# Decoder layer: feed-forward integers transposed by DMA, cross scores on four row tiles

## The chip, the cores and the metric

The kernel runs on one core of a Trainium2 chip. The metric is the device time of one execution in microseconds; the time before is the median of three runs. The core's engines are named as in the profile: PE (TensorE; PEld is its weight load), DVE (VectorE), ACT (ScalarE), POOL (GpSimd) and SP (SyncE, which issues most DMAs). PSUM is the memory PE writes to; it is used here as eight banks of 128 partitions by 512 floats.

## What is computed

One decoder layer for 32 sequences of 256 tokens and 256 features, in float32, with the norm after each residual sum:

```python
x = layernorm(x + self_attention(x))        # 16 heads of 64, 4 key/value heads, rotary, ALiBi, no mask
x = layernorm(x + cross_attention(x, ctx))  # 16 heads of 16, windows of 64 tokens, cell mask
x = layernorm(x + feed_forward(x))          # 256 -> 1024 -> 256, quantised
```

In cross attention the query in window w sees keys of the windows w-1 and w that lie not after it and have the same cell number. The scores of a head contract over only 16 features. In the feed-forward both operands of each product are quantised: the activations are scaled by 127 over the row's largest absolute value and rounded to whole numbers, the weights are rounded to -1, 0 and 1. Whole numbers up to 127 are exact in bfloat16, so these three products run in bfloat16.

```python
scale = 127.0 / clip(max(abs(x), axis=-1, keepdims=True), 1e-05)
xq = clip(round(x * scale), -128.0, 127.0) / scale
gate = silu(bitlinear(x, w_gate)); up = bitlinear(x, w_up)
return bitlinear(gate * up, w_down)
```

## The kernel before

All weights, rotary tables and the ALiBi rows are loaded once and stay on the core. The work is cut by batch (sequence), and each batch into many small parts, written as Python generators (`self_inputs`, `self_output`, `cross_inputs`, `cross_output`, `feed_forward`) and unit functions (`self_scores`, `self_turn`, `self_values`, `cross_scores`, `cross_exp`, `cross_turn`, `cross_values`, `cross_back`). A loop at the end of the kernel (L891 to L945) walks over "slots": two slots are a step, a batch has eight steps (16 slots), and in each slot every running generator goes on to its next `yield`; `yield 2` means "go on two slots later". So three batches are in work at a time: while the self scores of batch b run, batch b-1 is in its cross attention and feed-forward and batch b+1 has its inputs projected.

The order on PE, DVE and ACT is exactly the order in which the loop records the instructions. The orders on POOL and on SP are set by the scheduler. Each engine works its own instructions in order; a waiting instruction holds up all behind it.

PSUM tiles come from one pool of eight banks (`bank(...)`). A new tile takes over the bank that has been free longest, so its first writer waits for the last reader of the tile before. SBUF tiles come from `work(name, shape, bufs)`; with `bufs` 1 the next writer waits for the last reader of the one buffer.

The parts that the change touches:

- `cross_scores` (L648). A unit is one half of the query tokens (`qc`, 128 rows) and one half of the features (`ch`, 8 heads of 16). The features of 8 heads lie on 128 partitions. The keys stand in `kTz`, which is block diagonal: in each group of 64 partitions (4 heads) the key of head j stands in column block j, zeros elsewhere (`XHH` is 4). One matmul of 64 rows thus gives the scores of 4 heads side by side, 4 x 128 columns, in one bank. The two groups of 64 partitions are two row tiles of the PE array. Query half 0 sees 128 keys (2 matmuls of 128 queries). Query half 1 is two windows with different keys: 4 matmuls of 64 queries, two row by two column tiles. Eight DVE reductions (L668) then add the mask and find the row maxima. There are four units per batch, one in every second step.
- `cross_inputs` (L570), whose end (L637 to L640) copies the rotated keys into `kTz` by eight small DMAs. `kTz` is zeroed once, in `prepare_buffers` (L170).
- `feed_forward` (L766). POOL scales x2 and adds a large constant, which rounds (L783); DVE subtracts it and writes bfloat16 `xib` (L785). In the next slot PE transposes it in four blocks (L790) and ACT copies the result from PSUM to `xiT` (L794); in the slot after that the gate products start (L802). ACT's tanh (L816) and DVE (L817, L823) make the gated product in `gu`. For each half of the tokens (t = 0, 1) DVE finds the row maximum (L829) and the scales, POOL rounds (L838), and one slot later DVE writes the bfloat16 numbers into the lower part of `gu` itself (L843). One slot after the second of these, PE transposes half 0 in eight blocks (L849), ACT copies it (L851), and one slot later the down product runs (L855). Half 1 follows one slot behind that. Then the residual, the statistics, the norm and the store (L859 to L864).
- On SP's queue, in this order within a batch: the two copies inside `xvaug` (L631, L632), the next `xT` (L112), a rotary exchange `other<-psin` (L313, four DMAs each), the eight `kTz` copies (L640), an exchange `other<-qb` (L555), `ck_i` (L576), the residual input `xs` (L320), more exchanges, the store (L195) and the next context `cs` (L574).
- Other names used below: `s` and `p`, self scores and their softmax (L394, L410, L420); `t` and `pT`, its transpose and ACT's copy of it (L447, L452); `o`, values; `wo`, output product, added to the residual by DVE in L505 (`row`); `R`, the broadcast reciprocals; `proj`, projections (L331); `xt`, `xpT`, `xo`, `xoT`, the same for cross attention; `zoT` and `zT` (L205, L206), the transposed input of the cross output product `xw` (L755).

Of the kernel before, what the change touches and what calls it, by code (L numbers as in the profile page):

```python
# [9 lines left out]
F32 = mybir.dt.float32  # L10
BF16 = mybir.dt.bfloat16
I32 = mybir.dt.int32
AF = mybir.ActivationFunctionType
ALU = mybir.AluOpType
AX = mybir.AxisListType

P = 128
L = 256
# [32 lines left out]
def kernel(  # L51
# [33 lines left out]
    def ctile(shape, dtype, name):  # L85
        return const.tile(shape, dtype, name=name, tag=name)
# [3 lines left out]
    def bank(name, shape=(P, 512), dtype=F32):  # L90
        return ps.tile(list(shape), dtype, tag="b", name=name)
# [67 lines left out]
        t = ctile([P, (NT + 1) * XH * XE + 32 - XE], F32, f"xvaug{i}")  # L159
        xvaug_bufs.append(t)  # L160

    kTz = ctile([P, NDC, XHH, L], F32, "kTz")

    def prepare_buffers():
        nc.gpsimd.tensor_copy(cq_sb, cq_i)
# [404 lines left out]
    def cross_inputs(b):  # L570

        s = state[b]
        cs = work("cs", [P, NT, D], 1)
        nc.sync.dma_start(cs, cx[b].rearrange("(t p) d -> p t d", p=P))  # L574
        ck_i = work("ck_i", [P, L], 1, I32)
        nc.sync.dma_start(ck_i, cell_k[b].partition_broadcast(P))  # L576
        yield 4
        mvs = [stats(cs[:, t, :], "zc") for t in range(NT)]
        rstds = [rstd_of(mv, "zc") for mv in mvs]
        yield  # L580
        zc = cs
        for t in range(NT):
            last.append(partial(scaled, zc[:, t, :], cs[:, t, :], rstds[t]))
        ck = work("ck", [P, L], 1)
        nc.gpsimd.tensor_copy(ck, ck_i)
        yield 2
        zcT = work("tr", [P, NDC, L], 3)
        for t in range(NT):
            transposed(zcT[:, :, t * P : (t + 1) * P], zc[:, t, :], "zcT")


        s["mask"] = mask = work("mask", [P, NT, P])
        for rows_, t, k0 in ((slice(0, P), 0, 0), (slice(0, 64), 1, 64), (slice(64, P), 1, 128)):
            nc.gpsimd.tensor_scalar(
                mask[rows_, t, :], ck[rows_, k0 : k0 + P], cq_sb[rows_, b, t : t + 1], BIG, ALU.is_equal, ALU.mult
            )
        nc.gpsimd.tensor_tensor(mask, mask, base_sb, ALU.add)
        yield
        s["xv"] = xvaug_bufs[b % 2]
        xvaug = s["xv"][:, 0 : (NT + 1) * XH * XE].rearrange("p (t h e) -> p t h e", h=XH, e=XE)  # L600
        pk = bank("xk")
        for ch in range(NDC):
            for dc in range(NDC):
                nc.tensor.matmul(  # L604
                    pk[:, ch * L : (ch + 1) * L],
                    xkv_w[:, dc, ch * P : (ch + 1) * P],
                    zcT[:, dc, :],
                    start=(dc == 0),
                    stop=(dc == NDC - 1),
                )  # L610
        pair = biased(pk, K_, L)
        yield
        pv = bank("xv")
        for t in range(NT):
            for dc in range(NDC):
                nc.tensor.matmul(  # L616
                    pv[:, t * D : (t + 1) * D],
                    zcT[:, dc, t * P : (t + 1) * P],
                    xkv_w[:, dc, D : 2 * D],
                    start=(dc == 0),  # L620
                    stop=(dc == NDC - 1),
                )
        for t in range(NT):
            nc.vector.tensor_tensor(
                xvaug[:, t, :, 0:XHD],
                pv[:, t * D : (t + 1) * D].rearrange("p (h e) -> p h e", e=XHD),
                xbias[V_].rearrange("p (h e) -> p h e", e=XHD),
                ALU.add,
            )

        nc.sync.dma_start(xvaug[0:64, NT, :, :], xvaug[64:P, 0, :, :])  # L631
        nc.sync.dma_start(xvaug[64:P, NT, :, :], xvaug[0:64, 1, :, :])  # L632
        yield
        kT = work("tr", [P, NDC, L], 3)
        rotated(kT, *pair, 1, 0)
        yield 3
        for half in range(2):  # L637
            for j in range(XHH):
                rows_ = slice(half * 64 + j * XHD, half * 64 + (j + 1) * XHD)
                nc.sync.dma_start(kTz[rows_, :, j, :], kT[rows_, :, :])  # L640


# [5 lines left out]
    def cross_scores(b, i):  # L648
        s = state[b]
        qc, ch = cross_units[i]  # L650
        banks = [bank("xs") for _ in range(2)]
        for q0, q1, k0, _t in spans[qc]:
            for half in range(2):
                rows_ = slice(half * 64, (half + 1) * 64)
                nc.tensor.matmul(  # L655
                    banks[half].rearrange("p (h k) -> p h k", k=P)[q0:q1],
                    s["xqT", qc][rows_, ch, q0:q1],
                    kTz[rows_, ch, :, k0 : k0 + P],
                    start=True,
                    stop=True,  # L660
                )
        s["xnm", i] = [small("xnm", 4) for half in range(2)]
        for half in range(2):
            s["xp", i, half] = p = work("xp", [P, 512])
            for j in range(XHH):
                cols = slice(j * P, (j + 1) * P)

                nc.vector.tensor_tensor_reduce(  # L668
                    p[:, cols],
                    banks[half][:, cols],  # L670
                    s["mask"][:, qc, :],
                    -1.0,
                    3.0e38,
                    ALU.add,
                    ALU.min,
                    s["xnm", i][half][:, j : j + 1],
                )
# [88 lines left out]
    def feed_forward(b):  # L766
# [16 lines left out]
            nc.gpsimd.tensor_scalar(xi[:, t, :], x2[:, t, :], up[:, t : t + 1], MAGIC, ALU.mult, ALU.add)  # L783
        yield
        nc.vector.tensor_scalar(xib, xi, MAGIC, None, ALU.subtract)  # L785
        yield
        pt = bank("xiT", (P, NDC, L), BF16)
        for dc in range(NDC):
            for t in range(NT):
                nc.tensor.transpose(  # L790
                    pt[:, dc, t * P : (t + 1) * P], xib[:, t, dc * P : (dc + 1) * P], ident_b
                )
        xiT = work("xiT", [P, NDC, L], 1, BF16)
        nc.scalar.copy(xiT, pt)  # L794
        yield

        gu = work("gu", [P, NT, INNER], 1)

        def hidden(name, t, half):
            pg = bank("ff")  # L800
            for dc in range(NDC):
                nc.tensor.matmul(  # L802
                    pg,
                    xiT[:, dc, t * P : (t + 1) * P],
                    ff_w[name][:, dc, half * 512 : (half + 1) * 512],
                    start=(dc == 0),
                    stop=(dc == NDC - 1),
                )
            return pg
# [9 lines left out]
        for t in range(NT):  # L819
# [2 lines left out]
                cols = gu[:, t, half * 512 : (half + 1) * 512]  # L822
                nc.vector.tensor_tensor(cols, cols, pg, ALU.mult)  # L823
            yield
        d_ofs, hibs = [], []
        for t in range(NT):

            m = small("ffm", 1)
            nc.vector.tensor_reduce(m, gu[:, t, :], AX.X, ALU.max, apply_absolute_value=True)  # L829
            sh = small("ffsh", 1)  # L830
            nc.vector.tensor_scalar(sh, m, u_of[:, t : t + 1], QUANT_MIN, ALU.mult, ALU.max)
            hup = small("ffhup", 1)
            nc.vector.reciprocal(hup, sh)
            nc.vector.tensor_scalar(hup, hup, u_of[:, t : t + 1], 127.0, ALU.mult, ALU.mult)
            d_of = small("ffd", 1)
            nc.vector.tensor_scalar(d_of, sh, ff_scale["down"], None, ALU.mult)
            d_ofs.append(d_of)
            nc.gpsimd.tensor_scalar(gu[:, t, :], gu[:, t, :], hup, MAGIC, ALU.mult, ALU.add)  # L838
            yield

            gh = gu[:, t, :].rearrange("p (h n) -> p h n", h=2)
            hib = gu[:, t, :].bitcast(BF16).rearrange("p (h x n) -> p h x n", h=2, x=2)[:, :, 0, :]
            nc.vector.tensor_scalar(hib, gh, MAGIC, None, ALU.subtract)  # L843
            hibs.append(hib)
        yield
        for t in range(NT):
            pt = bank("hiT", (P, NIC, P), BF16)
            for ic in range(NIC):
                nc.tensor.transpose(pt[:, ic, :], hibs[t][:, ic // 4, ic % 4 * P : (ic % 4 + 1) * P], ident_b)  # L849
            hiT = work("hiT", [P, NIC, P], 1, BF16)  # L850
            nc.scalar.copy(hiT, pt)  # L851
            yield
            py = bank("ffo")
            for ic in range(NIC):
                nc.tensor.matmul(  # L855
                    py[:, 0:D], hiT[:, ic, :], ff_w["down"][:, ic, :], start=(ic == 0), stop=(ic == NIC - 1)
                )
            y = x2[:, t, :]
            nc.vector.scalar_tensor_tensor(y, py[:, 0:D], d_ofs[t], y, ALU.mult, ALU.add)  # L859
            mv = stats(y, "y")  # L860
            rstd = rstd_of(mv, "y")
            yield
            last.append(partial(scaled, y, y, rstd))
# [171 lines left out]
```

## Time and profile before

| | |
|---|---|
| median of three runs | 2324.79 us (2323.94 to 2325.04) |
| profiled execution | 2327.47 us |
| its span, first to last instruction | 2325.7 us |
| mean granted PE clock | 0.987 |
| ACT, copies hiT (L851) and xiT (L794) | 64.7 + 18.7 us busy |
| DVE, cross reductions (L668) | 225.9 us busy |
| DMA engines, queue of SP and ACT | 18.7% of 16 engines |

The span is the time between the first and the last instruction of the profiled execution; all rows of the profile belong to that execution, and a sum over rows is set against it. "Busy" of a group is the time covered by its instructions, where those of one group may overlap. In a timeline row the first number is the start within the span, the second how long the instruction or merged group lasted; brackets give idle time of the engine just before and what ended it. Names such as 64*128 behind a PE row are the rows and columns of the array tile that is used; "x8" is a number of records.

### The profile page before, as it was taken

Reading aid. Unit: us, or ns where it says so; the run is one execution under the profiler, and the core shown is the slowest. Engines: PE = TensorE matmul, PEld = TensorE weight load, DVE = VectorE, ACT = ScalarE, POOL = GpSimd, SP = SyncE. Lnnn points to the kernel's source line nnn. Section 1 sums busy time; section 2 is a strip of 40 time slices with the busy share of each in tenths; the row PEclk is TensorE's granted clock in tenths of the full one; section 3 lists DMA queues with packets and bytes.
Section 4 is the critical chain, followed back from the end, with each engine's and each line's share of the span. In section 5 each row is a group of like instructions: output and inputs, shape, how many; then the busy total and the mean of one; then the engine's idle time right before and its main releaser. Section 6 shows DMA issues by size and latency. Waiting matters only on the chain.

```text
span 2325.7 us, 54754 instructions
## 1 busy us (share of the span) xinstructions
PE 2246.9 (97%) x17637; PEld 1689.2 (73%) x17700; DVE 1701.3 (73%) x6949; ACT 1764.8 (76%) x5057; POOL 1124.2 (48%) x1851
## 2 busy tenths in 40 slices
PE   7999999999999999999999999999999999999985
PEld 5677777777777777777777777777777777777652
DVE  3767777777777777777777777777777777777765
ACT  2677777878777878777878777878777878777873
POOL 5344545445545545545445545445545444545432
PEclk9999999999999999999999999999999999999996
DMA  6311211112211111211111211112211111211000
GB/s 211 87 51 47 58 53 49 47 45 52 59 52 49 47 45 53 57 51 49 47 47 54 56 51 49 47 46 54 56 51 50 46 48 53 55 47 44 20 22 10
DMA packets 105407, 123.05 MB, mean 53 GB/s; under 512 B 21792, under 2 KB 74912, under 8 KB 105120
## 3 DMA queue, kind: packets, MB, share of 16 engines
q1 hardware_dynamic: 103424, 115.96, 18.7%
q10 hardware_dynamic: 1696, 3.57, 0.4%
q8 instruction: 142, 2.33, 0.4%
q14 instruction: 145, 1.19, 0.2%
HBM read 39.50 MB, written 8.39 MB: 21 GB/s over the span
## 4 chain that ended last, share of the span: by engine, by line
PE 78%; DVE 10%; ACT 8%; issue 1%; POOL 1%; DMA 1%; SPq 0%; ACTq 0%; POOLq 0%; DVEq 0%
PE proj L331 12%; PE s L394 10%; PE wo L495 10%; PE t L447 8%; PE o L464 8%; PE xt L693 4%; ACT p L420 4%; PE xs L655 4%; DVE gu L817 3%; PE xw L755 3%; PE xv L616 3%; PE ffo L855 3%; DVE p L410 2%; PE R L479 2%; PE xk L604 2%; PE v L363 2%
## 5 line engine op out<-in xcount | busy, mean ns | idle before, releaser
L420 ACT ACTIVATE p<-p,nm 128x256 f32<-128x256 f32 x1024 | 508.0, 498 | 168.6 <-DVE nm L410 164.7
L410 DVE CUSTOM_DVE_ANT_0 p<-s,alibi 128x256 f32<-128x256 f32 x1024 | 372.7, 420 | 180.5 <-PE s L394 180.4
L452 ACT COPY pT<-t 128x512 f32<-128x512 f32 x512 | 275.2, 591 | 127.1 <-PE t L447 126.8
L684 ACT ACTIVATE xp<-xp,xnm 128x128 f32<-128x128 f32 x1024 | 326.1, 394 | 5.9 <-DVE xnm L668 5.9
L394 PE MATMUL s<-kT,qT 64*128 64x256 f32 x2048 | 290.8, 402 | 0.0
L447 PE MATMUL t<-ident,p 128*128 128x128 f32 x2048 | 269.0, 273 | 3.2 <-ACT p L420 3.2
L447 PEld LDWEIGHTS t<-ident,p 128*128 128x128 f32 x2048 | 237.9, 141 | 31.4 <-ACT p L420 6.6
L331 PE MATMUL proj<-xT,wq_sb 128*128 128x256 f32 x1024 | 251.8, 389 | 0.0
L464 PE MATMUL o<-pT,v 128*64 128x256 f32 x2048 | 250.0, 385 | 0.0
L495 PE MATMUL wo<-wo_sb,oT 128*128 128x256 f32 x1024 | 245.3, 382 | 0.0
L668 DVE CUSTOM_DVE_ANT_0 xp<-xs,mask 128x128 f32<-128x128 f32 x1024 | 225.9, 286 | 2.9 <-PE xs L655 2.1
L495 PEld LDWEIGHTS wo<-wo_sb,oT 128*128 128x128 f32 x1024 | 189.4, 190 | 47.4 <-issue 22.7
L355 POOL TENSOR_TENSOR qT<-qT,other 128x512 f32<-128x512 f32 x128 | 162.9, 1273 | 120.6 <-DMA other<-psin 53.3
L394 PEld LDWEIGHTS s<-kT,qT 64*128 64x128 f32 x2048 | 176.5, 186 | 54.7 <-issue 23.5
L340 DVE TENSOR_TENSOR psin<-proj,rs_sb 128x512 f32<-128x512 f32 x160 | 110.2, 689 | 141.7 <-PE proj L331 141.7
L331 PEld LDWEIGHTS proj<-xT,wq_sb 128*128 128x128 f32 x1024 | 186.4, 191 | 32.8 <-issue 6.4
L464 PEld LDWEIGHTS o<-pT,v 128*64 128x64 f32 x2048 | 135.7, 136 | 98.3 <-issue 22.9
L420 ACT ACTIVATION_READ_ACCUMULATOR p<-p,nm 128x1 f32 x1024 | 192.6, 188 | 0.0
L695 ACT COPY xpT<-xt 128x512 f32<-128x512 f32 x256 | 153.2, 598 | 6.1 <-PE xt L693 4.2
L693 PE MATMUL xt<-ident,xp 128*128 128x128 f32 x1024 | 154.2, 274 | 0.0
L655 PE MATMUL xs<-kTz,xqT 64*64 64x512 f32 (+1 forms) x768 | 136.6, 611 | 5.0 <-POOL xqT L568 5.0
L817 DVE SCALAR_TENSOR_TENSOR gu<-gu,ff 128x512 f32<-128x512 f32 x128 | 82.3, 682 | 72.8 <-ACT gu L816 72.8
(156 smaller groups left out, 4528.2 us busy)
## 6 DMA issues: line engine op xcount, KB each, us to landing
other<-psin SPq DMA_DIRECT2D x640, 64.0 KB, 2.0
xT<-in_xt_dram SPq DMA_DIRECT2D x32, 256.0 KB, 2.7
xs<-in_x_dram SPq DMA_DIRECT2D x32, 256.0 KB, 2.7
cs<-in_ctx_dram SPq DMA_DIRECT2D x32, 256.0 KB, 2.7
other<-qb SPq DMA_DIRECT2D x64, 128.0 KB, 2.0
kTz<-tr SPq DMA_DIRECT2D x256, 32.0 KB, 2.0
other<-qb SPq DMA_DIRECT2D x128, 64.0 KB, 1.9
out_dram<-x SPq DMA_DIRECT2D x32, 256.0 KB, 2.2
```

The source lines that it names most:

```text
L331: nc.tensor.matmul(pq[:, c * L : (c + 1) * L], w[:, dc, c * P : (c + 1) * P], xT[:, dc, :], start=(dc == 0), stop=(dc == NDC - 1),)
L394: nc.tensor.matmul(banks[half][:, rr * L : (rr + 1) * L], qT[rows_, rr, qc * P : (qc + 1) * P], kT[rows_, kc, :], start=(rr == 0), stop=(r ...
L410: nc.vector.tensor_tensor_reduce(p[:, cols], banks[half][:, cols], alibi[:, 2 * (4 * kc + 2 * rp + rr) + half, :], -0.125, 3.0e38, ALU.add ...
L420: nc.scalar.activation(p[:, cols], p[:, cols], AF.Exp, bias=nm[:, rr : rr + 1], scale=-1.0, accum_out=s["sums", i // 2][:, (2 * rp + rr) * ...
L447: nc.tensor.transpose(pt[:, j * P : (j + 1) * P], p[half][:, rr * L + kk * P : rr * L + (kk + 1) * P], ident,)
L452: nc.scalar.copy(pT[half], pt)
L464: nc.tensor.matmul(po[half * HD : (half + 1) * HD, rp * L : (rp + 1) * L], s["v"][:, kk, (2 * kc + half) * HD : (2 * kc + half + 1) * HD], ...
L495: nc.tensor.matmul(py[:, 0:D], s["oT", qc, kc][:, r, :], wo_sb[:, 4 * kc + r, :], start=(kc == 0 and r == 0), stop=(kc == 1 and r == 3),)
L655: nc.tensor.matmul(banks[half].rearrange("p (h k) -> p h k", k=P)[q0:q1], s["xqT", qc][rows_, ch, q0:q1], kTz[rows_, ch, :, k0 : k0 + P], ...
L668: nc.vector.tensor_tensor_reduce(p[:, cols], banks[half][:, cols], s["mask"][:, qc, :], -1.0, 3.0e38, ALU.add, ALU.min, s["xnm", i][half][ ...
L684: nc.scalar.activation(p[:, cols], p[:, cols], AF.Exp, bias=s["xnm", i][half][:, j : j + 1], scale=-1.0)
L693: nc.tensor.transpose(pt[:, j * P : (j + 1) * P], p[:, j * P : (j + 1) * P], ident)
```

## The change

Cross scores: `kTz` has two column blocks in place of four, and the partitions are taken in four groups of 32 (2 heads) in place of two of 64 (4 heads). Each unit takes four banks, of which each holds 2 x 128 columns, and the matmuls name their tile of the array. Query half 0 is now 4 matmuls, query half 1 is 8. The DVE reductions stay eight, and read another bank for each pair of heads. The number of `kTz` DMAs stays eight.

Feed-forward: the PE transposes of `xib` and of the quantised hidden values, with the ACT copies behind them, are replaced by DMA transposes issued on SP: two for `xib` (one per token half), one for each half of the hidden values. The gate products start in the same slot as before. The hidden numbers go to a tile of their own, `hib`, with one buffer; `hiT` has two buffers in place of one. The down product of half 1 comes one slot after that of half 0 (it was two slots).

```diff
-    kTz = ctile([P, NDC, XHH, L], F32, "kTz")
+    kTz = ctile([P, NDC, 2, L], F32, "kTz")
...
-        for half in range(2):
-            for j in range(XHH):
-                rows_ = slice(half * 64 + j * XHD, half * 64 + (j + 1) * XHD)
+        for r in range(4):
+            for j in range(2):
+                rows_ = slice(r * 32 + j * XHD, r * 32 + (j + 1) * XHD)
                 nc.sync.dma_start(kTz[rows_, :, j, :], kT[rows_, :, :])
...
-        banks = [bank("xs") for _ in range(2)]
+        banks = [bank("xs") for _ in range(4)]
         for q0, q1, k0, _t in spans[qc]:
-            for half in range(2):
-                rows_ = slice(half * 64, (half + 1) * 64)
+            for r in range(4):
+                rows_ = slice(r * 32, (r + 1) * 32)
                 nc.tensor.matmul(
-                    banks[half].rearrange("p (h k) -> p h k", k=P)[q0:q1],
+                    banks[r][:, 0 : 2 * P].rearrange("p (h k) -> p h k", k=P)[q0:q1],
                     s["xqT", qc][rows_, ch, q0:q1],
                     kTz[rows_, ch, :, k0 : k0 + P],
                     start=True,
                     stop=True,
+                    tile_position=(r * 32, q0),
                 )
...
-                    banks[half][:, cols],
+                    banks[2 * half + j // 2][:, j % 2 * P : (j % 2 + 1) * P],
...
         nc.vector.tensor_scalar(xib, xi, MAGIC, None, ALU.subtract)
-        yield
-        pt = bank("xiT", (P, NDC, L), BF16)
-        for dc in range(NDC):
-            for t in range(NT):
-                nc.tensor.transpose(
-                    pt[:, dc, t * P : (t + 1) * P], xib[:, t, dc * P : (dc + 1) * P], ident_b
-                )
-        xiT = work("xiT", [P, NDC, L], 1, BF16)
-        nc.scalar.copy(xiT, pt)
-        yield
+        xiT = work("xiT", [P, NT, NDC, P], 1, BF16)
+        for t in range(NT):
+            nc.sync.dma_start_transpose(xiT[:, t, :, :], xib[:, t, :])
+        yield 2
...
-            gh = gu[:, t, :].rearrange("p (h n) -> p h n", h=2)
-            hib = gu[:, t, :].bitcast(BF16).rearrange("p (h x n) -> p h x n", h=2, x=2)[:, :, 0, :]
-            nc.vector.tensor_scalar(hib, gh, MAGIC, None, ALU.subtract)
-            hibs.append(hib)
-        yield
-        for t in range(NT):
-            pt = bank("hiT", (P, NIC, P), BF16)
-            for ic in range(NIC):
-                nc.tensor.transpose(pt[:, ic, :], hibs[t][:, ic // 4, ic % 4 * P : (ic % 4 + 1) * P], ident_b)
-            hiT = work("hiT", [P, NIC, P], 1, BF16)
-            nc.scalar.copy(hiT, pt)
-            yield
+            hib = work("hib", [P, INNER], 1, BF16)
+            nc.vector.tensor_scalar(hib, gu[:, t, :], MAGIC, None, ALU.subtract)
+            hiT = work("hiT", [P, NIC, P], 2, BF16)
+            nc.sync.dma_start_transpose(hiT, hib)
+            hiTs.append(hiT)
+        yield 2
+        for t in range(NT):
             py = bank("ffo")
```

The gate, up and down products read `xiT` and `hiTs[t]` in place of the former tiles.

More of the change, by code (lines that the diff above doesn't have):

```diff
@@ L803, in hidden @@
                     pg,
-                    xiT[:, dc, t * P : (t + 1) * P],
+                    xiT[:, t, dc, :],
                     ff_w[name][:, dc, half * 512 : (half + 1) * 512],
@@ L824, in feed_forward @@
             yield
-        d_ofs, hibs = [], []
+        d_ofs, hiTs = [], []
         for t in range(NT):
@@ L855, in feed_forward @@
                 nc.tensor.matmul(
-                    py[:, 0:D], hiT[:, ic, :], ff_w["down"][:, ic, :], start=(ic == 0), stop=(ic == NIC - 1)
+                    py[:, 0:D], hiTs[t][:, ic, :], ff_w["down"][:, ic, :], start=(ic == 0), stop=(ic == NIC - 1)
                 )
```

## The prediction

> **What bounds the kernel now.** First the page: engine totals, and the chain that ended last.
>
> ```profile
> PE 2246.9 (97%) x17637; PEld 1689.2 (73%) x17700; DVE 1701.3 (73%) x6949; ACT 1764.8 (76%) x5057; POOL 1124.2 (48%) x1851
> ...
> PE 78%; DVE 10%; ACT 8%; issue 1%; POOL 1%; DMA 1%; SPq 0%; ACTq 0%; POOLq 0%; DVEq 0%
> ```
>
> PE is the bound, but its busy time overlaps itself (matmul ends are modelled), so I price PE work by the distance between starts in the timeline. The chain of waits shows the pace: the same projection at 1084.67 and 1154.33 us, so a batch takes 69.65 us, and 32 of them are nearly the whole span. Within a batch PE stops once, for 0.39 us (row xw below). PE timeline of one batch (start, duration; a float matmul shows as two records):
>
> ```profile
> 1046.50 1.13 PE L394 MATMUL s<-kT,qT 64*128 64x256 f32 x8
> 1047.56 1.09 PE L655 MATMUL xs<-kTz,xqT 64*64 64x512 f32 x8
> 1048.58 1.04 PE L802 MATMUL ff<-ff_up,xiT 128*128 128x512 bf16 x4
> ...
> 1052.67 1.13 PE L755 MATMUL xw<-xo_w,zT 128*128 128x256 f32 x4 [0.39 <-ACT zT L206]
> ...
> 1061.83 1.13 PE L394 MATMUL s<-kT,qT 64*128 64x256 f32 x8
> 1062.80 1.02 PE L655 MATMUL xs<-kTz,xqT 64*128 64x512 f32 x4
> 1063.75 1.99 PE L495 MATMUL wo<-wo_sb,oT 128*128 128x256 f32 x8
> 1065.68 0.65 PE L709 MATMUL xo<-xpT,xvaug 128*32 128x64 f32 x32
> 1066.26 0.62 PE L849 MATMUL hiT<-ident_b,gu 128*128 128x128 bf16 x8
> 1066.72 1.95 PE L331 MATMUL proj<-xT,wkv_sb 128*128 128x256 f32 x8
> ```
>
> **Transposes off PE.** A set of 8 hiT transposes takes 1066.72 − 1066.26 = 0.46 us; two sets are 0.92, and the four xiT take 1107.74 − 1107.52 = 0.22. Per batch 1.14, times 32: **36 us**. (The group rows say 41.1 + 12.8 = 54 us of busy time; that counts overlap.) ACT loses 64.7 + 18.7 = 83 us of copies; ACT is not the bound, so I count nothing for them.
>
> **Cross scores.** Today a unit costs 1063.75 − 1062.80 = 0.95 us (two row tiles; query half 0) or 1048.58 − 1047.56 = 1.02 (two by two tiles; half 1). Afterwards the zeros shrink from 3 in 4 to 1 in 2: four row tiles at once, each with 256 columns to stream instead of 512. No row has four row tiles. The nearest is xo, four column tiles: 8 matmuls of 128 columns, 1024 columns in all, from 1084.03 to 1084.60, 0.57 us. The new unit also streams 4 x 256 = 1024 columns over four tiles (half 1: 8 x 256 over eight). Bound from below: 0.43 (half the present stream of 0.86). From above: s, which has the same 8 records of 256 columns and full-width weights on two tiles, 0.97: no gain. I take 0.60, near xo, because weight loads of different row tiles overlap in this trace: the eight half-width loads of a half-1 unit cover only 13.4 us / 64 = 0.21 us.
>
> Against it stands a rule: the Trainium skill, "TensorEngine Tiling (Array Packing)", Key Properties: changing the tiling mode drains the array. The trace has a price: s takes 1062.80 − 1061.83 = 0.97 when xs follows in its own mode (64*128), and 1047.56 − 1046.50 = 1.06 when another follows; call it 0.10. Half 0 now gains such a switch, half 1 had it. By the pure stream the gain is 0.95 − 0.60 = 0.35; by rule and row together 0.25. So 64 x 0.25 + 64 x 0.42 = 16 + 27 = **43 us**.
>
> **What does not arrive.** (1) In the feed-forward step the 0.39 us wait above is for ACT's zT copy, at the end of a run in which DVE is full (gate and up products, then all reductions, 1044.57 to 1055.6). PE arriving 0.42 earlier there just waits longer: 0.42 x 32 = **13 us** lost. (2) The second ffo moves from after xs (1081.94) into the slot of the second hiT set (1076.38). In the step of 1080.01 PE then reaches xw 1.07 + 0.60 + 0.90 + 0.31 + 0.57 + 1.83 = 5.28 us after s; ACT's zT copy ends 1085.68 − 1080.01 = 5.67 after it. 0.39 x 32 = **12 us** lost.
>
> **The DMA transposes.** Four per batch, on SP's queue: two of 64 KB (xiT) and two of 256 KB (hiT). The trace has no such transfer. Ordinary ones:
>
> ```profile
> other<-psin SPq DMA_DIRECT2D x640, 64.0 KB, 2.0
> xT<-in_xt_dram SPq DMA_DIRECT2D x32, 256.0 KB, 2.7
> ```
>
> Price T of a hiT transfer: the Trainium skill, "DMA: Bandwidth & Descriptors", Anatomy of one DMA, puts some 2.0 us on any transfer, and its Latency section measured 261 GB/s for one kernel's transposes: 262144 B / 261 = 1.0, so 3.0 by the rule. By the trace: queue q1 moved 103424 packets in 18.7% of 16 x 2325.7 us, 67 ns each; rows of 128 elements are 1024 packets, 64 per DMA engine, 4.3 us, plus 2.0: 6.3. If it goes in pieces of 16 elements (the program's transpose tile is 16 rows by 128 columns), 512 pieces x 67 ns = 34 us. I take **4.5 us**, between the first two, and keep 3 and 34 as ends.
>
> Where it is hidden:
>
> ```profile
> 1061.02 0.70 DVE L843 TENSOR_SCALAR gu<-gu 128x1024 bf16<-128x1024 f32 x1 [0.58 <-POOL gu L838]
> ...
> 1066.63 0.69 DVE L843 TENSOR_SCALAR gu<-gu 128x1024 bf16<-128x1024 f32 x1
> 1067.24 0.42 DVE L505 TENSOR_TENSOR row<-wo,xs 128x256 f32<-128x256 f32 x1
> ```
>
> - xiT: xib ends at 1105.49, the gate matmuls start at 1112.80. Two 64 KB transfers, 0.6 us apart, at 2.0 to 3.5 us land by 1109.6: free.
> - hiT of token half 0: written by 1061.72, needed by ffo at 1073.56: free up to T = 11.8. Half 1: written by 1067.32, needed at 1076.4: 9 us.
> - The new tile hib has **one buffer**: DVE's second hib waits until the first transfer has read it. That wait has 1066.63 − 1061.72 = 4.9 us of cover. Behind it on DVE stand row L505, the reciprocals, psin and the next four p reductions; the first PE casualty is s at 1070.13, which needs the PSUM bank that row L505 frees (1067.66), 2.5 us later, some 1.8 in the shorter new schedule. So PE loses T − 6.7 per batch once T exceeds 6.7; nothing at 4.5.
> - SP: the hiT transfers come after ck_i (1056.30) and before xs (1067.68) and psin (1069.51), the xiT ones between xvaug (1104.63) and xT (1107.71): gaps of 5 us and 3 us. A psin transfer behind the second hiT may land 1 to 2 us late; the key sum that waits for it is used slots later, and POOL is 48% busy. Nothing.
>
> **PSUM.** A cross unit now takes four of eight banks. The reuse distance shrinks by two: xs's third and fourth bank wait for ACT's pT copies (end 1099.73 where xs starts 1100.44), xo in the feed-forward step for xs's first bank (freed about 1050.0; PE arrives about 1050.2). These fit, narrowly. Nothing in the sum; the loss is a rival.
>
> **End of the kernel.** In the last batch nothing covers: xib to gate is 1.3 us now, about 3.5 then (+2); first hib (ends 2311.24) to second ffo (2317.48) becomes wait 4.5, second hib 0.65, transfer 4.5: 2320.9 (+3.5). **+5.5 us**.
>
> **Sum.** 2325.7 − 36 − 43 + 13 + 12 + 5.5 = 2277 span. The profiled execution took 2327.5, 1.8 more than its span; the median is 2324.8, 2.7 below that execution. So 2278.7 − 2.7: **2276 us**, 2.1% faster.
>
> **Rivals.**
> - A, four tiles don't help: s-like loading (0.97 per unit) or four-bank waits of 0.3 to 0.4 us eat the 43 us. For: no row has four row tiles; bank slacks are tenths. Against: the overlapping loads, xo. Then the stall of (1) goes too: 2325 − 36 + 12 + 5 + 6 (the switches) = about **2310**.
> - B, slower: the transfer of hiT through one hib buffer. PE loses T − 6.7 per batch; the 49 us gain is 1.5 per batch, so it decides from T = 8.2. At T = 10: 3.3 x 32 = 106, less 49, plus 11 more at the end: about **2390**. For: small pieces are dear in this trace, the form is unseen. Against: the 64 KB and 256 KB rows at 2.0 and 2.7.
> - C, the ACT relief counts: copies of 1.01 us stand ahead of pT where o waits. If both losses (1) and (2) vanish: **2250**.
> - D, the change does not do what it says: the transposes do leave PE and the zeros halve, in every batch; only "no change by offset" remains, **2325**.
>
> **Chances.** Forecast (2250 to 2300) 0.48; C and beyond 0.05; A (2300 to 2320) 0.12; D 0.05; B and other slow cases 0.30, most of it within 2330 to 2375, a tail beyond for T over 9. A measurement of this kernel tells 0.2%, 4.7 us. Faster 0.65, same 0.05, slower 0.30. Leaving out 0.05 below and 0.15 above gives 2245 to 2375; the likeliest case alone is 2250 to 2300.
>
> **What would show it.** L790, L794, L849 and L851 gone; xs of either half near 0.6 us from start to start, with s at 1.06 before every one; a batch period near 68.1 us; DMA transposes landing in about 4.5 us; zT waits ahead of xw near 0.8 and 0.4. Wrong if: DVE's second hib shows an idle time "<-DMA hiT" of microseconds and PE waits for row L505 (B); xs near 0.9, or PE waiting for DVE xnm or ACT pT (A).

## The result and the profile after

The kernel after takes 2287.4 us in the median of four runs (2286.42 to 2288.16), against 2324.65 us: ratio 0.984, 95% interval 0.982 to 0.985. That is 37 us less, and 11 us more than the forecast of 2276.

First the page of the kernel after: engine totals, the queue that carries SP's and ACT's transfers (packets, MB, share of 16 engines), and the engines' shares of the chain that ended last.

```profile
PE 2186.2 (96%) x17828; PEld 1653.7 (72%) x17828; DVE 1709.6 (75%) x6949; ACT 1692.1 (74%) x4961; POOL 1117.3 (49%) x1851
...
q1 hardware_dynamic: 189440, 136.95, 24.3%
...
PE 71%; DVE 12%; ACT 11%; DMA 2%; issue 2%; POOL 1%; SPq 0%; ACTq 0%; POOLq 0%; DVEq 0%
```

PE's busy time fell by 61 us, the span only by 39 (2325.7 to 2286.3). The chain points to where the rest went: ACT's share grew from 8 to 11% although ACT has 73 us less to do. PE now waits longer for something that ACT does late. The PE timeline of the kernel after shows it (start, duration; in brackets idle time and its releaser):

```profile
1060.79 1.14 PE L394 MATMUL s<-kT,qT 64*128 64x256 f32 x8
1061.86 0.71 PE L656 MATMUL xs<-kTz,xqT 32*128 32x256 f32 x8
1062.50 1.16 PE L532 MATMUL xq<-zT,xq_w 128*128 128x128 f32 x8
1063.50 0.38 PE L205 MATMUL zoT<-ident,on 128*128 128x128 f32 x2
...
1064.38 1.99 PE L331 MATMUL proj<-xT,wq_sb 128*128 128x256 f32 x8
1066.57 1.13 PE L757 MATMUL xw<-xo_w,zT 128*128 128x256 f32 x4 [0.19 <-ACT zT L206]
1067.53 1.04 PE L447 MATMUL t<-ident,p 128*128 128x128 f32 x8
...
1096.82 0.73 PE L656 MATMUL xs<-kTz,xqT 32*64 32x256 f32 x16
1097.49 1.04 PE L798 MATMUL ff<-ff_up,xiT 128*128 128x512 bf16 x4
...
1100.15 1.04 PE L798 MATMUL ff<-ff_up,xiT 128*128 128x512 bf16 x4
1101.93 1.13 PE L757 MATMUL xw<-xo_w,zT 128*128 128x256 f32 x4 [0.74 <-ACT zT L206]
1102.89 1.04 PE L447 MATMUL t<-ident,p 128*128 128x128 f32 x8
```

Read it from start to start: these two cross units cost 0.64 and 0.67 us, s ahead of them 1.07. Both zT waits are there. The first of these two steps in the kernel before, for comparison:

```profile
1081.94 1.05 PE L855 MATMUL ffo<-ff_down,hiT 128*128 128x256 bf16 x8
1082.82 1.06 PE L532 MATMUL xq<-zT,xq_w 128*128 128x128 f32 x8
1083.72 0.38 PE L205 MATMUL zoT<-ident,on 128*128 128x128 f32 x2
...
1084.60 1.99 PE L331 MATMUL proj<-xT,wq_sb 128*128 128x256 f32 x8
1086.43 1.03 PE L755 MATMUL xw<-xo_w,zT 128*128 128x256 f32 x4
1087.30 1.04 PE L447 MATMUL t<-ident,p 128*128 128x128 f32 x8
```

A bracket understates such a stall. The proj group ahead of xw takes 2.19 us against 1.83 before, and xw then takes 0.96 against 0.87: 0.45 us for a bracket of 0.19. The 0.1 us in xw itself goes with its weights: without a stall they start to load 0.21 us ahead of its first matmul (kernel before), in the stall only 0.01 us ahead.

What ACT does ahead of zT in the feed-forward step (the wait at 1101.93) of the kernel after, four exponentials first:

```profile
1099.85 1.26 ACT L686 ACTIVATE xp<-xp,xnm 128x128 f32<-128x128 f32 x4
1101.02 0.60 ACT L550 ACTIVATE qb<-xq,xbcol 128x128 f32<-128x128 f32 x2
1101.52 0.36 ACT L206 COPY zT<-zoT 128x256 f32<-128x256 f32 x1
```

The period, the mean distance of the down products of 25 batches, is 68.23 us against 69.65: 1.42 us per batch, 45 us in 32 batches. Span less 32 periods leaves 97 us before and 103 after, so 6 us went back at the two ends. Step by step, from start to start, per batch:

| step of the forecast | forecast | after | one part alone |
|---|---|---|---|
| transposes and the moved ffo, off PE | -1.14 | -1.15 | transposes alone: -1.15 |
| four cross units | -1.54 | -1.37 | tiles alone: -1.36 |
| mode switch, s ahead of half 0 | +0.20 | +0.19 | tiles alone: +0.19 |
| zT wait, feed-forward step | +0.42 | +0.34 | tiles alone: +0.35 |
| zT wait in the step that ffo left | +0.39 | +0.45 | transposes alone: +0.23 |
| xq, now directly behind xs | 0 | +0.10 | transposes alone: +0.09 |
| sum | -1.67 | -1.44 (period: -1.42) | -0.83 and -0.82 |

The "one part alone" column is read from the two runs that follow. The last view of the kernel after is its DMA transposes of hiT (time on SP's queue in ns, who waited for them, landing):

```profile
L839 SPq DMA_TRANSPOSE hiT<-hib x64: 1232/1245/1860, 223.9 to 2275.1; - x64
...
  PE ffo L845: 16.6, 4
  DVE hib L837: 2.5, 2
...
DMA to landing us min/median/max: 3.0/3.1/4.8
```

A transfer of 256 KB lands after 3.1 us; those of xiT, 64 KB each, after 2.4. PE waited for hiT 4 times in the whole kernel, DVE twice, all near the end.

### The profile page after: what moved, and what is told of

Read it like the earlier page. It is cut to its first block, busy times and chain, and to the rows that moved or that the text cites. A ratio compares the mean times of both kernels' runs of the same rounds, so it can differ in the third digit from the quotient of the medians.

```text
span 2286.3 us, 55642 instructions
## 1 busy us (share of the span) xinstructions
PE 2186.2 (96%) x17828; PEld 1653.7 (72%) x17828; DVE 1709.6 (75%) x6949; ACT 1692.1 (74%) x4961; POOL 1117.3 (49%) x1851
## 3 DMA queue, kind: packets, MB, share of 16 engines
q1 hardware_dynamic: 189440, 136.95, 24.3%
## 4 chain that ended last, share of the span: by engine, by line
PE 71%; DVE 12%; ACT 11%; DMA 2%; issue 2%; POOL 1%; SPq 0%; ACTq 0%; POOLq 0%; DVEq 0%
PE s L394 10%; PE proj L331 10%; PE wo L495 9%; PE t L447 8%; PE o L464 8%; ACT p L420 4%; DVE p L410 4%; PE xt L695 4%; DVE gu L813 3%; PE xw L757 3%; ACT xp L686 3%; PE xv L616 3%; PE ffo L845 2%; PE R L479 2%; PE xk L604 2%; PE v L363 2%
## 5 line engine op out<-in xcount | busy, mean ns | idle before, releaser
L566 POOL TENSOR_TENSOR qb<-qb,rx_sb 128x256 f32<-128x256 f32 (+1 forms) x96 | 87.7, 913 | 128.9 <-ACT xp L686 76.6
```

## Experiments

Times are medians; the kernel before was run beside each and took 2324.5 to 2324.7 us.

### The two parts alone

`transposes_alone` is the kernel before with the diff of `feed_forward` only. The old kTz leaves no room for more tiles, so the new ones lie in dead parts of gu (for hib `hib_in_gu` below shows that this costs nothing):

```diff
+            hib = gu[:, 0, :].bitcast(BF16)[:, 0:INNER] if t else work("hib", [P, INNER], 1, BF16)
...
+            hiT = gu[:, t, :].bitcast(BF16)[:, INNER : 2 * INNER].rearrange("p (c q) -> p c q", q=P)
```

> The kernel before with the DMA transposes of the feed-forward alone; the cross scores stay on two row tiles. (For want of room the second hib and both hiT lie in parts of gu that are dead by then, so no transfer waits for a buffer.) Theory (the steps of the prediction, with stalls that exist only where both parts meet): PE loses 1.14 us of transposes per batch and waits for no new thing, because cross scores of the old length leave ACT's zT copy in time: 36 us gained, 5.5 given back at the end, 2294 us; ahead of xw a wait only in the feed-forward step, 0.4 us as before. Rival (the two parts do not act on each other; the shortfall against the forecast is transfer contention or the ends): the two parts' gains, this one and that of the tiles alone, add up to the 37 us of the whole change, so this one gains about 20 to 25: 2300 to 2305.

`tiles_alone` has the diff of `kTz`, `cross_inputs` and `cross_scores` only.

> The kernel before with the cross scores on four row tiles alone; the feed-forward transposes stay on PE. Theory: per batch 2 x 0.21 (query half 0) and 2 x 0.37 (half 1) of PE time go, 1.16 us, and 0.35 come back as a longer wait for ACT's zT copy in the feed-forward step; the other zT wait does not arise, because the second down product still stands in that step. 0.81 x 32 = 26 us gained: 2299 us. Alone and alone then add up to 56 us against 37 together. Rival (parts are independent): 37 less the gain of the transposes alone, about 13 to 17 us: 2308 to 2312. Rival A of the prediction (four tiles bring new waits for banks or weight loads): under 10 us gained, PE waiting for DVE xnm or ACT pT ahead of xs or xo.

Measured: transposes alone 2307.3 us (ratio 0.9925, interval 0.9912 to 0.9937), tiles alone 2302.0 (0.9902, 0.9887 to 0.9917). The gains, 17 and 22.5 us, add up to 40 against 37 together: by the times, to within their noise of some 5 us, the parts are independent, and my theory of 56 against 37 fell. It fell in the transposes alone, of which I had expected 30 us. Its PE timeline says why:

```profile
1070.22 1.13 PE L394 MATMUL s<-kT,qT 64*128 64x256 f32 x8
1071.19 1.02 PE L655 MATMUL xs<-kTz,xqT 64*128 64x512 f32 x4
1072.15 1.16 PE L532 MATMUL xq<-zT,xq_w 128*128 128x128 f32 x8
1073.14 0.38 PE L205 MATMUL zoT<-ident,on 128*128 128x128 f32 x2
...
1074.03 1.99 PE L331 MATMUL proj<-xT,wq_sb 128*128 128x256 f32 x8
1075.99 1.13 PE L755 MATMUL xw<-xo_w,zT 128*128 128x256 f32 x4
1076.96 1.04 PE L447 MATMUL t<-ident,p 128*128 128x128 f32 x8
```

The ffo that stood between xs and xq (0.88 us) has left. That alone brings PE to zT too early, with cross units of the old length: proj takes 1.96 us instead of 1.83, xw 0.97 instead of 0.87. And xq, now directly behind xs, takes 0.99 instead of 0.90. That is 0.32 us per batch, 10 us, and no PE row shows a bracket for it.

The part of xq is no wait for ACT. Directly behind xs it takes 0.99 to 1.00 us here, in the kernel after and in xs_three_units, and also in exp_later, where the steady batches have no zT wait left; behind ffo or ff it takes 0.89 to 0.90. Behind ffo its first weights start to load 0.11 us ahead of its first matmul (kernel before, 1082.71 and 1082.82), behind xs at the same moment (kernel after, 1062.50). This looks like the change of mode on its way back, but no run tests that by itself.

What the two parts do to each other is the rest of the zT stall, 0.45 − 0.23 = 0.22 us per batch, 7 us: visible in the rows, not in the medians. The first line also shows the mode switch by its absence: s takes 0.97 ahead of two row tiles, and 1.06 to 1.07 in the same place of the tiles alone.

### ACT's order ahead of zT

In ACT's order four exponentials of the cross scores stand ahead of qb and the zT copy that PE waits for. `exp_later` moves their one line, in the kernel after; `exp_later_before` does the same in the kernel before.

```diff
-            if part == 1 and not odd:
-                cross(cross_exp, k, 0)
...
             for r in list(running):
...
                         r[0] += wait or 1
+            if part == 1 and not odd:
+                cross(cross_exp, k, 0)
```

> The kernel after with one line moved: the four ACT exponentials of the first half of a cross unit (L686, 1.26 us) are recorded behind the generators' steps, so that ACT does qb and the zT copy ahead of them. Theory (PE stops per batch for 0.45 and 0.74 us because these exponentials stand before zT on ACT): zT is ready 1.2 us earlier, both waits go, 1.19 x 32 = 38 us: 2249 us, period 67.0, and no wait ahead of xw over 0.1 us. Rival (DVE, which is full in those stretches, sets the pace a little later): the waits reappear at xt, wo or s and half or less is won: 2268 to 2287.

> The kernel before with the same one line moved, as a control. Theory: there is one zT wait of 0.39 us per batch there, 12.5 us in all: 2312 us. So the edit is worth some 25 us more on the kernel after than on the kernel before, and this difference is what the change left lying in ACT's order. Rival (the edit is worth the same on both, the change did not add the waits): equal gains on both.

Measured: 2248.5 us (0.967, 0.9657 to 0.9683) and 2305.6 us (0.9915, 0.9901 to 0.9928). The edit is worth 39 us on the kernel after and 19 on the kernel before. Timelines of ACT and PE in the feed-forward step of exp_later, then, from its page, the engines' shares of the chain that ended last:

```profile
1084.85 0.60 ACT L550 ACTIVATE qb<-xq,xbcol 128x128 f32<-128x128 f32 x2
1085.35 0.35 ACT L206 COPY zT<-zoT 128x256 f32<-128x256 f32 x1
1085.60 1.29 ACT L686 ACTIVATE xp<-xp,xnm 128x128 f32<-128x128 f32 x4
```

```profile
1085.15 1.04 PE L798 MATMUL ff<-ff_up,xiT 128*128 128x512 bf16 x3
1086.03 1.03 PE L757 MATMUL xw<-xo_w,zT 128*128 128x256 f32 x4
1086.89 1.04 PE L447 MATMUL t<-ident,p 128*128 128x128 f32 x8
```

```profile
PE 90%; DVE 4%; ACT 2%; DMA 2%; POOL 1%; issue 1%; SPq 0%; ACTq 0%; POOLq 0%; DVEq 0%
```

zT now comes directly behind qb, and the exponentials after it. The chain is PE for 90% and ACT for 2%. Against the kernel after, the ff group ahead of xw takes 0.88 us instead of 1.77, proj 1.83 instead of 2.19, both xw 0.1 less; 0.24 comes back at one o. So the waits ahead of xw came from ACT's order. In the kernel before, where only the feed-forward step shows a bracket, removing its 0.39 saved 0.66 us per batch (ff 1.43 to 0.88, xw 0.97 to 0.86), which is why the control gained 19 us and not the expected 12.5. The one line makes the change worth 57 us instead of 37 (2305.6 to 2248.5), and exp_later beats both kernels.

`exp_later_tiles` is exp_later with the transposes back on PE.

> The kernel before with the four row tiles and the exponentials moved behind zT on ACT, but with the feed-forward transposes on PE. With exp_later beside it, it prices the DMA transposes alone where no zT wait is in the way. Theory (gains and losses as read from the timelines: 69.00 us per batch of exp_later_before, less 1.37 of cross scores, plus 0.19 of mode switches): period 67.8, ends as before: 2265 to 2270 us, so that the DMA transposes are worth 17 to 22 us net. Rival (the DMA transposes gain nothing net, all of it is the tiles and ACT's order): 2250 or less.

Measured 2269.2 us (0.9764, 0.975 to 0.9779), period 67.83 in most batches. So the DMA transposes are worth 21 us net where no zT wait stands in the way; xq (+0.10), one o (+0.25) and the ends take part of what leaves PE.

`exp_later_pe_tail` uses PE and ACT for the transposes of the last two batches, placed directly behind hib.

> exp_later, with the feed-forward of the last two batches transposed on PE with ACT's copies, since nothing covers the DMA's latency there. Theory (the DMA transposes cost 5.7 to 6.8 us at the two ends of the kernel): 2242 to 2245 us. Rival (the ends are set by other things, PE's transposes and ACT's copies cost as much there): 2247 to 2250.

Measured 2249.2 us (0.9676, 0.9661 to 0.969): nothing gained, the rival's number. PE no longer waits for hiT's DMA (15.4 us in exp_later) but, four times and just as long, for DVE's hib (15.4 us). The 6 us at the ends exist, but this placement does not recover them; another was not tried.

### The one hib buffer

> The kernel after, with hib's one buffer out of play: the second token half's hib is written into the first half's part of gu, which is dead by then, so no hib waits for a transfer. Theory (the transfer of 3.1 us ends well inside the 5.0 us between the two hibs, so the buffer costs nothing in the steady batches and 2.5 us of DVE time in the last two): 2284 to 2288 us, period unchanged at 68.2. Rival B (the one buffer is what the forecast missed): 2276 or less.

`hib_in_gu` (the first line of the diff of the transposes alone, in the kernel after) took 2288.2 us (0.9842, 0.9827 to 0.9857), period 68.26: the buffer costs nothing. To see what a slower transfer would cost, the first half's hiT was transferred two times (again1, as below) or three times (again2, `range(2)`) in series, each transfer waiting for the one before it:

```diff
             nc.sync.dma_start_transpose(hiT, hib)
+            if t == 0:
+                for _ in range(1):
+                    nc.sync.dma_start_transpose(hiT, hib)
```

> The kernel after, with the first half's hiT transferred twice in a row, the second copy waiting for the first: hib is held about 2 x 3.1 = 6.2 us plus a little. Theory (the prediction's cover: 4.9 us on DVE, 6.7 before PE loses): DVE's second hib now shows 1.2 to 1.5 us of idle time '<-DMA hiT' in every batch, and PE loses nothing in the steady batches; about 3 us in each of the last two batches: 2290 to 2296 us, period 68.2 to 68.4. Rival (DVE has no slack there, so each us of its wait is one of PE's): 40 us more in the batches, 2330 or above.

> The same with three transfers in a row: hib is held some 9.3 to 9.6 us. Theory (PE loses T - 6.7): DVE idles about 4.5 us ahead of the second hib, PE loses 2.6 to 2.9 us per batch at wo, s or proj, 83 to 93 us, and about 12 at the end: 2380 to 2395 us. Rival (another slack of two us or more hides it, so that the prediction's deciding point of 8.2 us was far too low): under 2340.

> Three transfers in a row, but the second hib goes to gu and waits for none: what remains is SP's and the DMA engines' load, SP standing some 6 us longer ahead of xs, psin and the second hiT. Theory (the hib buffer is the only thing that a longer transfer costs): 2287 plus about 10 at the end, 2294 to 2300 us, period 68.2 to 68.4. Rival (psin and the second hiT behind the blocked queue are what costs): as again2_hib1, or half of its loss at least, 2335 or above.

| kernel | us | ratio, interval | period | span less 32 periods |
|---|---|---|---|---|
| again1_hib1 | 2304.1 | 0.9907, 0.9891 to 0.9924 | 68.54 | 109 |
| again2_hib1 | 2404.9 | 1.0344, 1.0325 to 1.0363 | 71.40 | 119 |
| again2_hib_gu | 2303.3 | 0.9907, 0.9892 to 0.9922 | 68.30 | 115 |

With three transfers and one buffer the kernel is slower than before; with three and no shared buffer it loses 16 us, 12 of them at the ends. So the buffer is the way in which a slow transfer would hurt in the batches; the longer occupied SP queue is not (period 68.30 against 68.23). DVE timeline of again2_hib1 in a batch of the milder kind, then PE's, there and in another batch:

```profile
1078.14 0.69 DVE L837 TENSOR_SCALAR hib<-gu 128x1024 bf16<-128x1024 f32 x1 [0.54 <-POOL gu L834]
1088.27 0.69 DVE L837 TENSOR_SCALAR hib<-gu 128x1024 bf16<-128x1024 f32 x1 [4.43 <-DMA hiT<-hib]
```

```profile
1086.66 1.13 PE L394 MATMUL s<-kT,qT 64*128 64x256 f32 x8
1089.35 1.95 PE L464 MATMUL o<-pT,v 128*64 128x256 f32 x16 [1.56 <-DVE row L505]
...
1231.01 3.68 PE L464 MATMUL o<-pT,v 128*64 128x256 f32 x16 [3.19 <-DVE row L505]
```

hib is held from 1078.83 to 1088.27, 9.4 us; DVE waits 4.4 of it. PE reaches o and waits for the bank that row L505 frees: from s to o 2.69 us instead of 1.06, 1.6 lost. The prediction's rule gives 9.4 − 6.7 = 2.7; here the cover is 7.8. The 3.2 us that again2 loses on average include batches like the second one, where the transfers ran late and PE, once stopped for 3.2 us, worked its next matmuls at nearly half speed (o 3.68 instead of 1.95).

In most batches of again1 hib is held 6.3 to 6.8 us and PE loses nothing (s to o 1.06). In seven the second transfer landed late and hib was held 7.6 to 8.0 us. There PE waited for the same row, ahead of s (us in total, times, longest):

```profile
PE s L394 <- DVE row L505: 2.9, 7, 0.6
```

The longest of them, at 1189.34 us, held hib for 8.04 us, and s took 2.34 us instead of 1.06: 1.28 lost, where the prediction's rule gives 8.04 − 6.7 = 1.34. So the rule holds where s waits for the bank, as it said; in again2 it is o, one group later, and the cover is longer by about the 1.06 us of s. The seven batches, with 6 us more at the ends, make 2304 of the expected 2290 to 2296.

### What a cross unit consists of

```diff
-                    banks[r][:, 0 : 2 * P].rearrange("p (h k) -> p h k", k=P)[q0:q1],
+                    banks[r][q0:q1, 0:P],
                     s["xqT", qc][rows_, ch, q0:q1],
-                    kTz[rows_, ch, :, k0 : k0 + P],
+                    kTz[rows_, ch, 0, k0 : k0 + P],
...
-                    banks[2 * half + j // 2][:, j % 2 * P : (j % 2 + 1) * P],
+                    banks[2 * half + j // 2][:, 0:P],
```

> The kernel after, with each cross score matmul streaming one column block of kTz (128 columns) in place of two; the scores of every second head are left out, and the reductions read the first block twice. It asks what the 0.64 us of a cross unit consist of. Stream theory (the prediction's floor of 0.43 for the stream of two 256-column records in each tile, plus 0.21 of loads and mode change that nothing hides): a unit takes 0.42 to 0.45 from start to start; of the 0.84 us per batch half comes back as longer zT waits in two of the four steps: 2270 to 2278 us. Load theory (the eight weight loads set the time, the stream is hidden): a unit stays at 0.58 to 0.66: 2284 to 2288 us.

Measured 2382.5 us (1.0237, 1.022 to 1.0254), 95 us slower than the kernel after: neither theory. The disputed size itself came out clearly:

```profile
1067.19 0.47 PE L656 MATMUL xs<-kTz,xqT 32*64 32x128 f32 x16
1067.60 1.04 PE L798 MATMUL ff<-ff_up,xiT 128*128 128x512 bf16 x4
```

A unit takes 0.40 to 0.44 us from start to start, so a block of 128 columns costs 0.22 and what remains is 0.21, as the stream theory had it. The rest is something else. ACT waits 3.3 us for POOL's rstd_zo, since POOL stands at qT for an exchange. The timeline of POOL, then of SP's queue, in xs_one_block:

```profile
1068.11 1.27 POOL L355 TENSOR_TENSOR qT<-qT,other 128x512 f32<-128x512 f32 x1 [7.06 <-DMA other<-psin]
1069.47 0.22 POOL L185 TENSOR_SCALAR rstd_zo<-mv_zo 128x1 f32<-128x1 f32 x1
```

```profile
1055.67 2.03 SPq L640 DMA_DIRECT2D kTz<-tr  x3
...
1062.71 0.64 SPq L640 DMA_DIRECT2D kTz<-tr  x1
1063.45 0.53 SPq L112 DMA_DIRECT2D xT<-in_xt_dram  x1
1064.09 2.49 SPq L313 DMA_DIRECT2D other<-psin  x4
```

Four of the eight copies to kTz now stand ahead of xT and psin (presumably those of its second block, which nothing reads any more); in the kernel after all eight come behind psin. `xs_three_units` keeps two blocks in the last unit of a batch, and with it SP's order:

> As xs_one_block, but only the first three of a batch's four cross units stream one block (the scores of every second head are left out in these three); the last unit streams both, so that SP's queue keeps the order of the kernel after. In xs_one_block SP issued four of the kTz copies ahead of xT and psin, psin landed late, and POOL, ACT and PE waited. Theory (that order, not the shorter cross unit, made xs_one_block 95 us slower than the kernel after): three units at 0.40 to 0.45 us, 0.22 less each; one of them stands ahead of a zT wait that takes its gain back: 0.44 x 32 = 14 us gained, 2270 to 2278 us. Rival (cross units this short themselves bring the stall at zoT, SP's order being innocent): above 2300, with PE waiting for ACT on ahead of zoT.

Measured 2272.6 us (0.9779, 0.9763 to 0.9796). Three units at 0.40 to 0.44 us, 0.20 of it back at the proj ahead of xw, period 67.80 in the batch compared. So three short units per batch are innocent, and SP's changed order, with what it set off, cost xs_one_block about 110 us (2382.5 − 2272.6). That the fourth short unit had no part in it is not shown by itself.

## Why the prediction was right, and where it was not

- **Transposes, mode switch.** 1.14 and 0.20 us per batch forecast, 1.15 and 0.19 measured. The price of 0.10 for a change of mode, read from the rows of s, held ahead of the new units; what happens inside PE at such a change no row shows.
- **Cross units.** The step "I take 0.60, near xo" was too low: 0.61 to 0.68 measured, on average 0.64. Its floor of 0.43 for the stream is confirmed (twice 0.22); the part that nothing hides is 0.21 and not 0.17, and what it consists of stays open. Over four units 0.17 us, 5 us in the kernel: the largest error of the sum.
- **Lost at zT.** Both losses came, at 0.34 and 0.45 instead of 0.42 and 0.39. The mechanism, ACT's copy at the end of its queue, is shown by exp_later. The first is smaller because the unit ahead of it gained less (0.35 us). That the second came so near is in part luck: PE was ready for xw 5.42 us after s and not 5.28, which shortens the wait, but zT ended at 5.73 and not 5.67, and the forecast had nothing for the 0.09 us that the stalled xw itself is longer. "What would show it" named brackets near 0.8 and 0.4; they read 0.74 and 0.19, and the second misleads.
- **Missed.** xq's 0.10 us, 3 us in all: with ffo gone it stands directly behind xs. The forecast charged the change of mode ahead of the row tiles and put nothing for the group behind them.
- **The transfer.** T was the term most mis-sized: 4.5 taken, 3.1 measured, next to the estimate of 3.0 that the Trainium skill, "DMA: Bandwidth & Descriptors", led to. (The fixed 2.0 us in it are measured there on transfers that GpSimd issues; for SP's they agree with the 64 KB rows of psin, 2.0.) The packet price of 67 ns was wrong for these packets. The queue's totals show 86016 more packets for (24.3% x 2286.3 − 18.7% x 2325.7) x 16 = 1931 us, 22 ns each. T did not decide, as both values are under the cover. But it fed rival B, which held most of the 0.30 for slower. B's mechanism is real (again2_hib1). Its T − 6.7 was met where s waited (again1_hib1); where o waited the cover was about one us longer.
- **Rivals A and C.** A had no effect beyond 5 us: four tiles work, and no row L505 or pT wait for banks came up in the steady batches. C, ACT's relief, did not come by itself: removing 83 us of copies left the exponentials ahead of zT.
- **Ends.** 5.5 us forecast, 6 measured.

Sum: 0.25 us per batch short (8 us), half a us at the ends. (The period of 68.1 that the prediction named shares out its 49 us, 5.5 of which belong to the end; its steps give 69.65 − 1.67 = 67.98.) The span was 9.3 us above the forecast's 2277, and the remaining 2 of the 11 us lie between span and median.

## What to carry to other kernels

When work leaves a bound engine, price how much earlier it arrives at each following wait, up to the next one that has slack, and look at which groups become neighbours; and price the stall from start to start of the groups around it, since the bracket showed only 40 to 75% of it here. Then look at what stands ahead of the releasing copy in its engine's order: here one moved line was worth as much as the whole change. Before replacing a single buffer's reader by a slower one, measure the cover between its two writes.

## What the runs showed of the hardware

A PE that stops for some 2 to 3 us mostly works at half speed afterwards. Three windows of xs_one_block, where PE waits ahead of zoT and xw; the columns are window, length, busy us of PE, PEld, DVE, ACT and POOL, granted clock, DMA share and GB/s:

```profile
1069.00:1071.40 2.40, 0.54 (x6) 0.34 (x4) 2.40 (x18) 0.66 (x2) 2.03 (x5) 1.00 0.26 54
...
1073.30:1075.30 2.00, 1.08 (x3) 0.17 (x2) 1.93 (x4) 2.00 (x9) 1.19 (x2) 0.50 0.00 0
...
1079.00:1081.00 2.00, 2.00 (x18) 1.39 (x18) 0.67 (x3) 1.17 (x2) 1.63 (x3) 1.00 0.01 4
```

The clock goes from 1.00 to 0.50 and is back at 1.00 some 7 us later; in between t takes 1.71 us instead of 0.88. Of the 28 stops ahead of o in again2_hib1, the 12 of up to 1.8 us were never followed by a slow o; of the 16 from 2.2 to 3.5 us 14 were (2.7 to 3.7 us instead of 1.95), and those of 2.83 and 2.94 were not. The Trainium skill, "TensorE: Matmul & The Clock Gate", Part 1, names an activity window of some 3.4 us that runs freely. That could be why stops of one length end differently; but most of these stops are shorter than that window, and no run here shows it, so the link stays open.

So a stall has a second price, and it is part of how a late psin grew to 110 us: the mean granted clock was 0.969 in xs_one_block and 0.985 in the kernel after. By an estimate from these two, with 1.00 and 0.50 as the only states, that is some 80 us more at half clock, worth up to 40 us.

Each DMA transpose takes 1.23 us of SP's queue, against some 0.6 for an ordinary issue there (four of psin in 2.46 to 2.49); four per batch are 5 us. In the batches of this kernel that time cost next to nothing: two more of them in again2_hib_gu moved the period from 68.23 to 68.30.
